# Layer 0's last state-space group: its squares summed on TensorE in the output product's PSUM bank, and a later share of the GLU stream

## The chip, the cores and the metric

The program runs on one core of a Trainium2 chip. Its time is the device time of one execution in microseconds (us). The engines are TensorE (PE; its weight loads are PEld), VectorE (DVE), ScalarE (ACT), GpSimd (POOL) and SyncE (SP), whose queue issues most of the transfers.

## The reference

Four layers act on a residual stream of 4 sequences of 512 tokens with 256 features. Layer 0 is a Mamba-2 mixer and then a SwiGLU. Only this part is changed:

```python
proj = einsum('bld,pd->blp', x, W_in)            # 2048 gate, 2304 x/B/C, 32 dt
hBC  = silu(causal_conv4(...)); xs, B, C = split(hBC)
dt   = softplus(dt + dt_bias);  dA = exp(-exp(A_log) * dt)
h_t  = dA_t * h_(t-1) + (dt_t * x_t) outer B_t   # 32 heads of 64, state 128
y    = (h . C) + D * xs
g    = y * silu(gate)
g    = g * rsqrt(mean(g*g over 2048) + 1e-5) * norm_w
out  = einsum('bli,di->bld', g, W_out)
```

Layer 1 is a latent attention and a product-key mixture with its own GLU; layers 2 and 3 are not touched.

## The kernel before

Tokens lie in 16 tiles of 128, four to a sequence. Everything is fp32.

**The mixer** is the generator `mamba_pieces`. It works in 16 groups `i` of 8 heads: `b = i // 4` is the sequence, `g = i % 4` the quarter of the heads. A group has four chunks `t` of 128 tokens; chunk (15, 2) below is group 15's third. A chunk takes these steps, by their lines in the profile:

- `before`: transposes of x into a "tr" bank (L429, TensorE), times dt (`xdt`, L431, VectorE).
- `products`: a scan over the decays, `G` (L415, VectorE, in program order).
- `before_gpsimd`, issued one chunk ahead: `G` times C·B (L449, GpSimd) and `xw` (L452, GpSimd).
- `within`: C times the state (L470, TensorE), times `eb` into `y` (L471, VectorE), `y` plus D·x (L472, GpSimd); the state's update (L478 TensorE, L483 and L484 VectorE); the product within the chunk (L488, TensorE), added to `y` (L493) and gated (L494, both VectorE); the squares `sq` of `y` (L496, ScalarE), which GpSimd adds in two halves to the running sums `ssq` (L500, L501; L498 for the sequence's first group).
- `project_out`, one chunk behind: `y` times W_out into a "tr" bank (L509, TensorE), added to `acc` (L515, VectorE).

After a sequence's last chunk TensorE sums `ssq` over the partitions with a column of ones (L520), `rsqrt` is taken of the sums (L90 ScalarE, L91 VectorE), the four tiles of `acc` are scaled into the residual (L152), and `part_done` lets `layernorm` run for that sequence.

While group `i` runs through its chunks, the input products of group `i + 1` (L134 with `w_in`) are made between them. Group 15 has no follower, so no such products lie between its chunks.

**The GLU stream** is `glu_units`: two units of layer 0's GLU for four sequences and the first unit of layer 1's GLU for sequences 0 and 1. A piece is four 128x512 products, gate and up, into "mm" banks (L134 with `wu`), or eight 128x256 products back (L212) into a "tr" bank, added to the residual (L158).

**`weave`** takes the next piece of the stream whose share of its stated total is smaller: 630 for the mixer, 207 for the GLU. Each `yield` names its piece's cost. The tile framework's scheduler then sets the order on each engine; an engine works strictly in that order and waits on semaphores.

**PSUM** has 8 banks: 4 "mm", 2 "tr", 2 "acc" (`Ctx.ps`). **SBUF**: `y` has 3 buffers, `sq` 2, `ssq` 1. The weights of layer 1 are loaded by the SP queue (L53) into memory that layer 0 has given up. ScalarE's queue issues the load of `psw` (L791), which stands ahead of its square root (L90).

Of the kernel before, what the change touches and what calls it, by code (L numbers as in the profile page):

```python
# [15 lines left out]
P = 128  # L16
NB, SEQ, DM = 4, 512, 256
NT = NB * SEQ
NTILE = NT // P
TPB = SEQ // P  # L20
# [62 lines left out]
def v3(ap, b):  # L83
    return ap.rearrange("p (a b) -> p a b", b=b)


def rsqrt(c, pool, out, in_, scale):

    s = c.tile(pool, list(in_.shape), "rsq")
    c.nc.scalar.activation(s, in_, AF.Sqrt, bias=c.eps, scale=scale)  # L90
    c.nc.vector.reciprocal(out, s)  # L91
# [55 lines left out]
def add_scaled(c, t, part, w=None):  # L147

    x = c.x[:, t, :]
    if w is None:  # L150
        return c.nc.vector.tensor_add(x, part, x)
    return c.nc.vector.scalar_tensor_tensor(x, part, w, x, ALU.mult, ALU.add)  # L152
# [93 lines left out]
def mamba_pieces(c, a, ws, open_pool):  # L246
# [4 lines left out]
    nc, tc = c.nc, c.tc  # L251
# [94 lines left out]
    pb, pg2, pool = open_pool("m_b", 2), open_pool("m_g", 2), open_pool("m_t", 2)  # L346
    seqs, groups, chunks, w_in, Gs = {}, {}, {}, {}, {}
# [5 lines left out]
    def sequence(b):  # L353

        tokens = slice(b * SEQ, (b + 1) * SEQ)
        BT = c.tile(pb, [P, SEQ], "BT", bufs=1)
        CT = c.tile(pb, [P, SEQ], "CT")
        for k, out in ((16, BT), (17, CT)):
            pc = c.ps()
            project(c, pc, w_bcd, slice((k - 16) * P, (k - 15) * P), tokens)  # L360
            taps = causal_conv(pool, pc, k, out)
            yield 1.7
            taps()
        pt, pcb = c.ps("tr"), c.ps("acc")
        for t in range(TPB):
            cols = slice(t * P, (t + 1) * P)
            nc.tensor.transpose(pt[:, cols], BT[:, cols], c.ident)
            nc.tensor.matmul(pcb[:, cols], lhsT=BT[:, cols], rhs=CT[:, cols], start=True, stop=True)
        Btok = c.tile(pb, [P, TPB, P], "Btok")
        CB = c.tile(pb, [P, TPB, P], "CB")  # L370
        nc.scalar.copy(Btok, v3(pt, P))
        nc.scalar.copy(CB, v3(pcb, P))
        acc = c.tile(pb, [P, TPB, DM], "acc")
        ssq = c.tile(pb, [P, TPB, 2, P], "ssq", bufs=1)
        seqs[b] = CT, Btok, CB, acc, ssq
        yield 1.3
# [68 lines left out]
    def before_gpsimd(i, t):  # L445
        b, g = i // 4, i % 4
        chunk = chunks[i, t]
        G, xdt = chunk[:2]
        nc.gpsimd.tensor_mul(G, G, seqs[b][2][:, t, :][:, None, :].to_broadcast([P, HG, P]))  # L449
        if t < TPB - 1:  # L450
            chunk[2] = xw = c.tile(pool, [P, 512], "xw")
            nc.gpsimd.tensor_mul(  # L452
                v3(xw, HD), v3(xdt, HD), by_head(after[:, b * TPB + t, g * HG : (g + 1) * HG])
            )

    state = {}

    def within(i, t):

        b, g = i // 4, i % 4  # L460
        CT, Btok, CB, acc, ssq = seqs[b]
        G, xdt, xw, xD, eb = chunks.pop((i, t))
        tt, hs, cols = b * TPB + t, slice(g * HG, (g + 1) * HG), slice(t * P, (t + 1) * P)
        y = c.tile(pool, [P, 4, P], "y", bufs=3)
        if t > 0:
            S = state[i]
            yb = c.ps("acc")
            for k in range(4):
                ks = slice(k * P, (k + 1) * P)
                nc.tensor.matmul(yb[:, ks], lhsT=S[:, ks], rhs=CT[:, cols], start=True, stop=True)  # L470
            nc.vector.tensor_mul(y, v3(yb, P), eb)  # L471
            nc.gpsimd.tensor_add(y, y, xD)  # L472
        n = 4 * i + t + 1
        if n < 64:
            before_gpsimd(n // 4, n % 4)
        if t < TPB - 1:
            pst = c.ps()
            nc.tensor.matmul(pst, lhsT=Btok[:, t, :], rhs=xw, start=True, stop=True)  # L478
            if t == 0:
                S = state[i] = c.tile(pool, [P, 512], "S")  # L480
                nc.scalar.copy(S, pst)
            else:
                nc.vector.tensor_mul(v3(S, HD), v3(S, HD), by_head(etot[:, tt, hs]))  # L483
                nc.vector.tensor_add(S, pst, S)  # L484
        ya = c.ps("acc")
        for h in range(HG):
            part = slice(h % 2 * HD, (h % 2 + 1) * HD)
            mm = nc.tensor.matmul(  # L488
                ya[part, h // 2 * P : (h // 2 + 1) * P],
                lhsT=xdt[:, h * HD : (h + 1) * HD], rhs=G[:, h, :], start=True, stop=True,  # L490
            )
            tc.keep_in_program_order(mm)
        tc.keep_in_program_order(nc.vector.tensor_add(y, v3(ya, P), y if t > 0 else xD))  # L493
        nc.vector.tensor_mul(y, y, groups[i][3][:, :, cols])  # L494
        sq = c.tile(pool, [P, 4, P], "sq")
        nc.scalar.activation(sq, y, AF.Square)  # L496
        if g == 0:
            nc.gpsimd.tensor_add(ssq[:, t], sq[:, :2], sq[:, 2:])  # L498
        else:
            nc.gpsimd.tensor_add(ssq[:, t], ssq[:, t], sq[:, :2])  # L500
            nc.gpsimd.tensor_add(ssq[:, t], ssq[:, t], sq[:, 2:])  # L501
        return y

    def project_out(i, t, y):
        b, g = i // 4, i % 4
        acc, ssq = seqs[b][3:]
        po = c.ps("tr")[:, :DM]
        for k in range(4):
            nc.tensor.matmul(  # L509
                po, lhsT=y[:, k, :], rhs=groups[i][1][:, k, :], start=(k == 0), stop=(k == 3)  # L510
            )
        if g == 0:
            nc.scalar.copy(acc[:, t, :], po)
        else:
            nc.vector.tensor_add(acc[:, t, :], po, acc[:, t, :])  # L515
        if g == 3 and t == TPB - 1:
            pss = c.ps()[:, :TPB]
            for u in range(TPB):
                for k in range(2):
                    nc.tensor.matmul(  # L520
                        pss[:, u : u + 1], lhsT=ssq[:, u, k, :], rhs=c.ones[:, :1],
                        start=(k == 0), stop=(k == 1),
                    )
            rs = c.tile(pb, [P, TPB], "rs")
            c.eps = c.eps5
            rsqrt(c, pb, rs, pss, 1.0 / 2048.0)
            for u in range(TPB):
                add_scaled(c, b * TPB + u, acc[:, u, :], rs[:, u : u + 1])
            c.part_done(b)
# [19 lines left out]
    behind = None  # L549
    for i in range(16):  # L550
        for t in range(TPB):
            if t == 1 and i % 4 == 3 and i < 15:
                yield from sequence(i // 4 + 1)
            taps = []
            for k in ((0, 1), (2,), (3,), ())[t] if i < 15 else ():
                taps.append(group(i + 1, k))
                yield 3.4
            n = 4 * i + t + 1
            if n < 63:
                decays((n + 1) // 4, (n + 1) % 4)  # L560
            if n < 64:
                before(n // 4, n % 4)
            yield 0.5
            for tap in taps:
                tap()
            y = within(i, t)
            if n < 63:
                products(n + 1)
            yield 2.6
            if behind:  # L570
                project_out(*behind)
                yield 1.7
            behind = i, t, y
    project_out(*behind)


# [28 lines left out]
def layer0(c, a, x_in, con):  # L605

    with ExitStack() as stack:
        open_pool = lambda name, bufs, **kw: stack.enter_context(
            c.tc.tile_pool(name=name, bufs=bufs, **kw)
        )  # L610
        c.weights = open_pool("m_w", 1)
        unit = c.tile(c.weights, [P, 3072], "wu")
        ws = c.tile(open_pool("m_ws", 1), [P, 762], "ws")
        first_loads(c, a, x_in, con, ws, unit)
        for b in range(NB):
            layernorm(c, b)
            c.step(True)
        glu = open_pool("g0", 1)

        def glu_units():  # L620
            same = dict(bufs=5, out_tag="tr")
            yield from glu_pieces(c, glu, [unit], loaded=True, last=False, **same)
            yield from glu_pieces(c, glu, [a["g0_units"][1]], first=1, **same)

            yield from glu_pieces(
                c, glu, [a["g1_units"][0]], last=False, seqs=[0, 1], **same
            )

        c.parts(2, lambda b: layernorm(c, b, c.xn[b * SEQ : (b + 1) * SEQ, :]))
        weave(  # L630
            c,
            (mamba_pieces(c, a, ws, open_pool), 630.0, 0.0),
            (glu_units(), 207.0, 0.0),
        )

# [1220 lines left out]
```

## Time and profile before

| | us |
|---|---|
| median of 3 runs | 3200.73 (3199.61 to 3208.17) |
| the profiled execution | 3132.11 |
| its span | 3130.3 |
| TensorE busy | 3075.6 (98% of the span) |
| VectorE, ScalarE, GpSimd busy | 1816.2, 1258.1, 650.8 |
| granted TensorE clock, mean | 0.993 |

The profiled execution is one run: 1.8 us lie around its span, and it took 68.6 us less than the median of the timed runs. Durations below are of this execution. TensorE's ends are modelled, so starts are the safer figures. An fp32 product shows as two records, so "x8" is four products. "Waits" lists who waited for whom; the "timeline" lists instructions in order with the idle time before them in brackets; "windows" give busy time and granted clock of a stretch.

### The profile page before, as it was taken

To read this page: it belongs to the slowest core of one execution; us is meant where nothing else is said; L and a number is where in the kernel's file an instruction comes from. 1 tells how busy PE (TensorE), PEld (TensorE's weight loads), DVE (VectorE), ACT (ScalarE), POOL (GpSimd) and SP (SyncE) were. 2 spreads that over 40 slices of the span, in tenths; PEclk is the share of its full clock that TensorE was granted. 3 is DMA by queue.
4 is the path that set the end of the run, shared out by engine and by line. 5 is a ranking of instruction groups with operands and counts; after the bars stand their busy time and mean duration, and the time that the engine had idled before them with its cause. 6 is when DMAs were issued, how large, how long until landed. Compare 5 with 4: busy or idle time off the path is not lost.

```text
span 3130.3 us, 35680 instructions
## 1 busy us (share of the span) xinstructions
PE 3075.6 (98%) x12502; PEld 1886.1 (60%) x12502; DVE 1816.2 (58%) x4644; ACT 1258.1 (40%) x2916; POOL 650.8 (21%) x517
## 2 busy tenths in 40 slices
PE   8999999999899999999999999999999999999999
PEld 5566566566656555555676656656566655555555
DVE  5777778777777787777656555455555422222222
ACT  4434435444466666667425433333333311111111
POOL 0465655556300133331233000000000000000000
PEclk9999999999999999999899999999999999999999
DMA  3233323232221154543232000000000000000000
GB/s 124 86 101 121 100 93 111 85 124 87 88 60 52 45 132 96 127 120 116 66 110 88 1 21 8 1 28 1 21 1 1 21 21 21 21 21 21 0 0 27
DMA packets 89090, 185.12 MB, mean 59 GB/s; under 512 B 14192, under 2 KB 57216, under 8 KB 84176
## 3 DMA queue, kind: packets, MB, share of 16 engines
q1 hardware_dynamic: 74448, 135.05, 13.4%
q0 software_dynamic: 14176, 47.01, 6.1%
q8 instruction: 99, 1.62, 0.2%
q10 hardware_dynamic: 288, 0.79, 0.1%
q14 instruction: 79, 0.65, 0.1%
HBM read 160.92 MB, written 12.98 MB: 56 GB/s over the span
## 4 chain that ended last, share of the span: by engine, by line
PE 87%; DVE 7%; POOL 2%; ACT 2%; DMA 1%; issue 1%; SPq 0%; ACTq 0%; DVEq 0%; POOLq 0%
PE mm L134 34%; PE acc L212 9%; PE mm L655 8%; PE mm L142 5%; PE acc L1165 4%; PE acc L671 4%; PE tr L509 3%; PE tr L1157 2%; PE tr L782 2%; PE tr L212 2%; PE acc L918 2%; PE acc L488 1%; PE mm L1495 1%; PE acc L932 1%; DVE cy L280 1%
## 5 line engine op out<-in xcount | busy, mean ns | idle before, releaser
L134 PE MATMUL mm<-xnT,wu 128*128 128x512 f32 x2128 | 951.2, 595 | 0.2
L134 PEld LDWEIGHTS mm<-xnT,wu 128*128 128x128 f32 x2128 | 400.4, 191 | 461.9 <-issue 438.5
L662 ACT ACTIVATE pr<-pr,nm 128x128 f32<-128x128 f32 (+3 forms) x512 | 285.7, 558 | 294.7 <-DVE nm L658 292.3
L202 DVE TENSOR_TENSOR hT<-sg,mm 128x512 f32<-128x512 f32 x176 | 120.4, 684 | 393.4 <-PE mm L134 388.4
L201 ACT ACTIVATE sg<-mm 128x512 f32<-128x512 f32 x176 | 104.6, 595 | 579.7 <-PE mm L134 579.5
L658 DVE CUSTOM_DVE_ANT_0 pr<-mm,late 128x128 f32<-128x128 f32 (+3 forms) x512 | 245.4, 482 | 93.4 <-PE mm L655 91.1
L212 PE MATMUL acc<-wu,hT 128*128 128x256 f32 x1280 | 287.1, 380 | 1.4 <-DVE x L158 1.4
L212 PEld LDWEIGHTS acc<-wu,hT 128*128 128x128 f32 x1280 | 241.4, 190 | 49.6 <-issue 17.2
L1036 POOL DMA_INDIRECT e<-in_p_experts,ids x128 | 130.7, 1021 | 477.9 <-DVE x L152 354.3
L134 PE MATMUL mm<-xnT,w_in 128*128 128x512 f32 x512 | 228.5, 593 | 0.1
L280 DVE SCALAR_TENSOR_TENSOR cy<-mm,ws,cy 128x509 f32<-128x509 f32 (+2 forms) x216 | 159.7, 745 | 65.4 <-ACT cy L276 61.8
L655 PE MATMUL mm<-kf,qf 128*128 128x128 f32 (+3 forms) x512 | 178.9, 449 | 2.3 <-DVE nm L658 1.3
L655 PE MATMUL mm<-k,q 128*128 128x128 f32 (+3 forms) x512 | 176.5, 434 | 1.0 <-DVE q L1130 1.0
L449 POOL TENSOR_TENSOR G<-G,CB 128x1024 f32<-128x1024 f32 x64 | 152.8, 2388 | 93.7 <-DVE G L415 93.7
L435 ACT ACTIVATE xD<-xc,ws 128x128 f32<-128x128 f32 x256 | 84.1, 391 | 196.2 <-POOL y L472 186.6
L134 PEld LDWEIGHTS mm<-xnT,w_in 128*128 128x128 f32 x512 | 96.7, 190 | 107.9 <-issue 101.5
L152 DVE SCALAR_TENSOR_TENSOR x<-acc,cw,x 128x256 f32<-128x256 f32 x128 | 61.9, 483 | 153.7 <-PE acc L212 153.6
L1165 PE MATMUL acc<-PT,V 128*128 128x512 f32 (+3 forms) x512 | 149.1, 433 | 0.0
L415 DVE TENSOR_TENSOR_SCAN G<-G,eye 128x1024 f32<-128x1024 f32 x64 | 146.8, 2295 | 0.0
L1130 DVE TENSOR_SCALAR q<-mm,bias 128x512 f32<-128x512 f32 x64 | 48.0, 750 | 165.2 <-PE mm L134 165.2
L782 PEld LDWEIGHTS tr<-con,pr 128*128 128x128 f32 x640 | 81.4, 143 | 90.9 <-ACT pr L775 29.1
L782 PE MATMUL tr<-con,pr 128*128 128x128 f32 x640 | 122.8, 283 | 10.1 <-ACT PT L786 4.7
(337 smaller groups left out, 4936.1 us busy)
## 6 DMA issues: line engine op xcount, KB each, us to landing
G<-own SPq DMA_DIRECT2D x64, 512.0 KB, 4.2
w_in<-in_m_units SPq DMA_DIRECT2D x16, 1024.0 KB, 5.4
eb<-since SPq DMA_DIRECT2D x96, 128.0 KB, 4.0
wu<-in_o_units SPq DMA_DIRECT2D x8, 1536.0 KB, 6.7
wo<-in_m_units SPq DMA_DIRECT2D x16, 512.0 KB, 3.8
psw<-pes SPq DMA_DIRECT2D x128, 64.0 KB, 3.2
wu<-in_g_units SPq DMA_DIRECT2D x4, 1536.0 KB, 6.9
wu<-in_f_units SPq DMA_DIRECT2D x4, 1536.0 KB, 7.3
```

The costliest lines, as they stand in the source:

```text
L134: c.nc.tensor.matmul(out, lhsT=w[:, d, cols], rhs=c.xnT[:, d, tokens], start=(d == 0), stop=(d == 1))
L142: c.nc.tensor.matmul(out, lhsT=c.xnT[:, d, tokens], rhs=w[:, d, cols], start=(d == 0), stop=(d == 1))
L212: nc.tensor.matmul(po[:, j, :], lhsT=hT[k][:, (t + j) * P : (t + j + 1) * P], rhs=wd[:, k, :], start=(i == 0), stop=(i == per - 1),)
L280: nc.vector.scalar_tensor_tensor(y[:, j:], src[:, : SEQ - j], conv[:, k, 3 - j : 4 - j], y[:, j:], ALU.mult, ALU.add,)
L415: tc.keep_in_program_order(nc.vector.tensor_tensor_scan(flat, flat, eye.rearrange("p h t -> p (h t)"), 0.0, ALU.mult, ALU.add))
L449: nc.gpsimd.tensor_mul(G, G, seqs[b][2][:, t, :][:, None, :].to_broadcast([P, HG, P]))
L655: nc.tensor.matmul(sc, lhsT=q[:, i * P : n], rhs=k[:, :n], start=True, stop=True)
L658: nc.vector.tensor_tensor_reduce(out=pr, in0=sc, in1=late[:, SEQ - n :], scale=1.0, scalar=-NEG, op0=ALU.add, op1=ALU.min, accum_out=nm,)
L662: nc.scalar.activation(pr, pr, AF.Exp, bias=nm, scale=-1.0, accum_out=total)
L782: nc.tensor.transpose(pt[:, (i - j) * P : (i - j + 1) * P], prs[s][i][:, j * P : (j + 1) * P], c.ident)
L1036: nc.gpsimd.indirect_dma_start(out=e, out_offset=None, in_=a["p_experts"], in_offset=bass.IndirectOffsetOnAxis(ap=ids[:, t, k : k + 1], ax ...
L1165: nc.tensor.matmul(z[:, j * P :], lhsT=head["V"][:, j, h, :], rhs=head["PT"][:, j, j * P :], start=(j == 0), stop=(j == TPB - 1),)
```

## The change

There are three edits, all in layer 0.

1. In group 15 alone, GpSimd no longer adds the squares to `ssq`. Instead `project_out` sums, for each chunk, the two blocks of `ssq` (groups 12 to 14) and the four blocks of `sq` with six products of one column, in column 256 of the bank that holds that chunk's output product. ScalarE copies the column to a new tile `sums`, from which `rsqrt` reads.
2. In group 15, two yields of each chunk name 2.5 more, and the mixer's total in `weave` goes from 630 to 650, so that the GLU stream moves later against the mixer, and goes on during group 15.
3. The third GLU unit (layer 1's) takes its L212 banks from "mm" and not from "tr".

```diff
-    state = {}
+    state, sums = {}, []
...
         if g == 0:
             nc.gpsimd.tensor_add(ssq[:, t], sq[:, :2], sq[:, 2:])
-        else:
+        elif i < 15:
             nc.gpsimd.tensor_add(ssq[:, t], ssq[:, t], sq[:, :2])
             nc.gpsimd.tensor_add(ssq[:, t], ssq[:, t], sq[:, 2:])
-        return y
+        return y, sq
...
-    def project_out(i, t, y):
+    def project_out(i, t, y, sq):
         b, g = i // 4, i % 4
         acc, ssq = seqs[b][3:]
-        po = c.ps("tr")[:, :DM]
+        bank = c.ps("tr")
+        po = bank[:, :DM]
...
             nc.vector.tensor_add(acc[:, t, :], po, acc[:, t, :])
+        if i == 15:
+            if t == 0:
+                sums.append(c.tile(pb, [P, TPB], "sums", bufs=1))
+            parts = [ssq[:, t, k, :] for k in range(2)] + [sq[:, k, :] for k in range(4)]
+            for k, part in enumerate(parts):
+                nc.tensor.matmul(
+                    bank[:, DM : DM + 1], lhsT=part, rhs=c.ones[:, :1], start=(k == 0),
+                    stop=(k == 5),
+                )
+            nc.scalar.copy(sums[0][:, t : t + 1], bank[:, DM : DM + 1])
         if g == 3 and t == TPB - 1:
-            pss = c.ps()[:, :TPB]
+            if i == 15:
+                pss = sums[0]
+            else:
+                pss = c.ps()[:, :TPB]
...
-            yield 0.5
+            alone = 2.5 if i == 15 else 0.0
+            yield 0.5 + alone
...
-            y = within(i, t)
+            y, sq = within(i, t)
...
-            yield 2.6
+            yield 2.6 + alone
...
-                c, glu, [a["g1_units"][0]], last=False, seqs=[0, 1], **same
+                c, glu, [a["g1_units"][0]], last=False, seqs=[0, 1], bufs=5, out_tag="mm"
...
-            (mamba_pieces(c, a, ws, open_pool), 630.0, 0.0),
+            (mamba_pieces(c, a, ws, open_pool), 650.0, 0.0),
```

In the changed file the six products are L523, the copy is L527, and L509 and L515 become L510 and L516; below, L509 and L515 keep their old names.

## Prediction

> **What bounds the kernel now.** The page first: TensorE is busy nearly throughout, so only its own work and the holes in it count.
>
> ```profile
> PE 3075.6 (98%) x12502; PEld 1886.1 (60%) x12502; DVE 1816.2 (58%) x4644; ACT 1258.1 (40%) x2916; POOL 650.8 (21%) x517
> ```
>
> Next the windows, to find the holes. In layer 0 they lie at its start (75 to 100 us) and, most of all, at its end. TensorE's busy time and clock there:
>
> ```profile
> 780.00:785.00 5.00, 2.98 (x26) 1.86 (x24) 3.35 (x3) 2.38 (x6) 2.81 (x3) 1.00 0.68 201
> 785.00:790.00 5.00, 4.40 (x13) 3.64 (x14) 4.96 (x6) 1.47 (x4) 4.92 (x4) 0.68 0.16 57
> ...
> 800.00:805.00 5.00, 3.41 (x25) 2.29 (x24) 5.00 (x6) 0.74 (x2) 3.87 (x3) 1.00 0.00 0
> 805.00:810.00 5.00, 2.52 (x14) 2.30 (x16) 4.39 (x6) 0.63 (x1) 2.75 (x2) 0.73 0.47 131
> ```
>
> The first pair after the length is TensorE, the fifth GpSimd, then the clock. TensorE has holes, and its clock falls after them, while GpSimd is nearly full. Third, TensorE's timeline at these places, with each hole and its releaser:
>
> ```profile
> 785.60 2.66 PE L509 MATMUL tr<-wo,y 128*128 128x256 f32 x8 [2.62 <-DVE acc L515]
> ...
> 802.82 1.99 PE L509 MATMUL tr<-wo,y 128*128 128x256 f32 x8 [1.41 <-DVE acc L515]
> 807.48 2.07 PE L470 MATMUL acc<-CT,S 128*128 128x128 f32 x8 [2.66 <-DVE S L484]
> ...
> 812.90 1.40 PE L520 MATMUL mm<-con,ssq 128*128 128x1 f32 x12
> ...
> 816.91 0.60 PE L520 MATMUL mm<-con,ssq 128*128 128x1 f32 x4 [0.35 <-POOL ssq L501]
> ...
> 825.07 1.13 PE L142 MATMUL mm<-wu,xnT 128*128 128x256 f32 x4 [1.85 <-DVE sg L166]
> ```
>
> The four holes before 818 add up to 7.04 us. At half clock, 785.60 to 792.7 and 807.48 to 811.07, the groups took 2.66, 4.68, 2.07 and 1.66 us where their full-clock neighbours take 1.99, 3.62, 1.06 and 1.09: 3.3 us lost. VectorE is only the messenger. Fourth, GpSimd's and VectorE's timelines:
>
> ```profile
> 801.06 1.92 POOL L500 TENSOR_TENSOR ssq<-ssq,sq 128x256 f32<-128x256 f32 x1 [2.26 <-ACT sq L496]
> 803.05 0.73 POOL L501 TENSOR_TENSOR ssq<-ssq,sq 128x256 f32<-128x256 f32 x1
> 803.74 2.35 POOL L449 TENSOR_TENSOR G<-G,CB 128x1024 f32<-128x1024 f32 x1
> ```
> ```profile
> 803.88 2.75 DVE L483 TENSOR_TENSOR S<-S,etot 128x512 f32<-128x512 f32 x1
> ```
>
> GpSimd idles for a chunk's squares with the next G behind it, and L483 (0.68 us at 770.23, when alone) ends only as L449 ends; the state, L484 and TensorE's L470 come after it. The bound of group 15 is thus the loop through GpSimd.
>
> **What the Trainium skill says.** "SBUF — State Buffer", section "SBUF: two separate sides": VectorE with two SBUF inputs and GpSimd hold one port pair exclusively, each for a whole instruction. The trace agrees (2.75 against 0.69 above). "TensorE: Matmul & The Clock Gate", Part 1: an idle window of about 3.4 us halves the clock until a busy window has passed. The trace shows half clock for about 3.3 us, but after idle stretches of only 2.62 and 2.66 us. "PSUM — Partial Sum Buffer", the rule under bank collisions: guard by bank, not by address. No trace here shows a collision, but in the built program the first L523 of each chunk does wait for that chunk's L515, which reads the same bank.
>
> **The change part by part.** I set the built order of the changed program against these durations. Zero is the start of L429 after the last `w_in` products, 767.63 in the trace.
>
> 1. *GLU pieces moved.* Before, two L212 blocks (3.45 us each) lie after zero. In the changed order it is two `wu` blocks (3.5 each) and two L212 blocks: 13.9 against 6.9, so zero itself comes 7.0 us earlier. On TensorE alone this is work moved, not saved; it pays by filling holes.
> 2. *L500, L501 of group 15 gone.* Eight instructions, about 10 us on GpSimd (0.73 to 2.70 each), off the loop. Chunk (15, 0)'s own G is not helped, since group 14's sums stay.
> 3. *L523 added.* Each chunk has six products of one column, 12 records; 12 records of L520 took 1.40 us. Four chunks: 5.6, less the four removed pairs (8 products, 1.9): +3.7 us on TensorE.
> 4. *Filling.* TensorE's work from zero to the last L523, from row starts (L429 0.44, L470 0.89, L478 0.95, L488 1.03, L509 1.83, blocks as above, 1.4 per six L523, 1.9 for layer 1's first products), is 50.8 us. Before, the end of L520 is at 817.51, that is 49.9, of which 39.5 is work at full clock; 39.5 + 7.0 + 3.7 + 0.9 for a product now ahead gives about the same.
> 5. *Waits that remain.* The 2.62 hole goes: y of (14, 3) is done at 15.4 as before, but TensorE comes to L509 at 18.8, not 15.3, since a `wu` block lies ahead. The L484 hole goes: the second L212 covers it. **A new wait appears**: L523 of (15, 0) stands ahead of L488 and L212 on TensorE and waits for L515 of (15, 0), which VectorE makes only after L493, L494 and the 2.28 us scan. TensorE gets there at 31.5, L515 ends at about 33.8: 2.5 us with the semaphore, with L488, the second L212 and the next L470 queued behind, and through L488 VectorE's L493. The later three L523 groups have 5 to 6 us or other products ahead; I give them and the last y together 0.9. Total 54.2.
> 6. *End of the squares.* 54.2 less 7.0 is 47.2 against 49.9: **2.7 us earlier**.
> 7. *After it.* ScalarE now makes a copy (0.3), and its `psw` issue (1.59 before, then beside the wait), table load (1.28) and root come in line behind: squares to root about 3.5 us, against 2.3. From the root VectorE still needs 4.5 us to L166. So the L142 that waited 1.85 us is reached 2.7 - 1.3 = **1.4 us earlier**, with a longer hole, about 4 us, since only 4.3 us of products (6.0 before) cover it.
> 8. *Start of layer 0.* The total of 650 also reorders its start: the first L212 now comes after the transposes, so VectorE's L158 no longer stands ahead of a convolution tap and the two scans. They began at 90.82 and may begin about 1.4 us sooner; at the end of that chain TensorE waited 3.54 us for `xw`. I take **1.4 us** (bounds 0 and 3.5).
> 9. *Costed at nothing.* Elsewhere in layer 0 the pieces shift by up to two; TensorE's other waits from 110 to 765 are 7 us in all, so at most that is gained, and as much may be lost: plus or minus 3. The GLU's weight loads (6.9 us to land) have over 12 us of products between last and first use. ScalarE's copies fit its idle time. Banks: L212 on "mm" competes with four products, no `w_in` among them after zero. The SP queue's L53 for layer 1 now also waits for the second L212 (39.9), first used at 47: covered by 7 us for a 385 KB load that goes first. Layers 1 to 3 keep their order.
>
> Sum: 1.4 + 1.4 = 2.8 us gained. The two half-clock stretches are already in the sum as gone; the new holes of 2.5 and about 4 us are of the size that brought them, and each would cost at most 1.65. I let them cost 0.3 together, since the later work also waits for other engines there, and take 2.5: 3129.6 for the profiled execution in place of 3132.11. The timed runs lie 68.6 us higher, I assume unchanged: **3198.2 us**.
>
> **Rivals.** A difference of 0.3% (9.6 us) is about what a measurement of this kernel can tell from no change.
>
> *Clean fill* (0.22): the L523 wait proves short, VectorE being freed of the port conflicts; all of 7.04 + 3.3 - 3.7 = 6.6 us at the end and 3.5 at the start are gained, 10.1, and with it some small waits: 3189. For it: GpSimd's 10 us. Against: the scan stands ahead of L515 in VectorE's order.
>
> *The bank's wait becomes the bound* (0.16, slower): each L523 waits for its L515, at 2.5 us in four places 10 us, three new half-clock stretches 5, and 3.7 of products, 18.7, against 10.3 taken away: 8.4 us longer, 3209; with the longer root, 1.3, 3210.4, just past 0.3%. It decides if TensorE comes to every L523 over 2 us before VectorE's L515. For it: the order. Against: L212 and L509 lie between in (15, 1).
>
> *It doesn't do what it says*: the GLU stream would run dry before group 15. The built order speaks against it, with four blocks after zero; this lies within the likeliest case, near 3201.
>
> **How the numbers follow.** The likeliest case (0.62), with plus or minus 3 for the other waits, 1.65 for each half-clock stretch and the bounds of the start, reaches 3191.5 to 3207 and lies within 0.3%. Faster by over 0.3% is the clean fill, 0.22; slower the bank's wait, 0.16. The range for 8 in 10, stretched to most of both rivals: 3186 to 3211.
>
> **What would show it.** In the profile after: no hole at the L509 of (14, 3); no L500 or L501 in group 15; L523 six times four, about 1.4 us each; a hole of some 2.5 us at the first L523, released by L515; L483 near 0.7 us in chunk (15, 2); a longer hole at L142 after the root, released by L166; the wait for `xw` near 100 us down to about 2. I am wrong if the end of the squares comes over 5 us earlier or any later than before, if TensorE's other waits in layer 0 grow by more than 3 us, or if the time moves in layers 1 to 3.

## The result, and the profile after

The changed kernel takes 3198.87 us (median of 22 runs, 3193.73 to 3209.55), the kernel before 3205.04 beside it (22 runs, 3196.41 to 3214.94). The ratio is 0.9979, 95% interval 0.9971 to 0.9986: **6.7 us faster (4.5 to 9.3)**, within the 0.3% that the prediction called no change. The forecast was 2.5 us.

The page of the kernel after, engines (lines after L507 carry numbers one to seventeen higher than before: L509 is L510, L515 is L516, L791 is L808):

```profile
PE 3099.3 (97%) x12534; PEld 1898.2 (59%) x12534; DVE 1820.1 (57%) x4644; ACT 1257.2 (39%) x2918; POOL 637.9 (20%) x509
```

TensorE has the 32 added records (12534 against 12502), GpSimd eight instructions fewer. This execution is 72 us longer than the one profiled of before. That is not the change's doing: layers 1 to 3, whose instructions are the same, took between 2246 and 2321 us in the traces of this study whatever the kernel (2321.3 us here, 2250.1 in another trace of the same changed kernel), and the kernel before has a median of 3131 us in one group of runs and of 3193 to 3205 in the others. So the traces are compared in layer 0.

Windows there (length, then TensorE, weight loads, VectorE, ScalarE, GpSimd; then the clock, the DMA share and GB/s):

```profile
785.00:790.00 5.00, 5.00 (x37) 3.84 (x36) 4.90 (x7) 0.00 (x0) 3.46 (x2) 1.00 0.00 1
790.00:795.00 5.00, 2.67 (x17) 1.75 (x15) 3.60 (x4) 1.91 (x5) 1.58 (x2) 1.00 0.19 55
795.00:800.00 5.00, 4.40 (x33) 3.86 (x34) 4.53 (x7) 0.16 (x1) 4.03 (x2) 0.81 0.00 0
...
825.00:830.00 5.00, 5.00 (x17) 2.84 (x16) 3.17 (x9) 2.14 (x11) 0.00 (x0) 0.66 0.31 105
```

The holes of group 15 are gone at 785, but a new one stands at 790 to 795, and the clock is low after it and again at 825. TensorE's timeline of the kernel after names them (start, length, engine, line, operation, tiles, form, records, and in brackets the idle time ahead and what ended it):

```profile
795.60 0.61 PE L523 MATMUL tr<-con,ssq 128*128 128x1 f32 x4 [2.93 <-DVE acc L516]
796.07 1.03 PE L523 MATMUL tr<-con,sq 128*128 128x1 f32 x8
797.03 1.09 PE L488 MATMUL acc<-G,xdt 128*64 128x128 f32 x16
798.05 5.41 PE L212 MATMUL mm<-wu,hT 128*128 128x256 f32 x16
...
814.90 1.02 PE L134 MATMUL mm<-xnT,wu 128*128 128x512 f32 x2
815.76 0.50 PE L523 MATMUL tr<-con,ssq 128*128 128x1 f32 x4
816.12 1.03 PE L523 MATMUL tr<-con,sq 128*128 128x1 f32 x8
...
824.58 1.32 PE L142 MATMUL mm<-wu,xnT 128*128 128x256 f32 x4 [3.02 <-DVE sg L166]
825.70 3.43 PE L134 MATMUL mm<-xnT,wu 128*128 128x512 f32 x4
```

The first L523 waits 2.93 us for L516, which reads its bank. Then L212 takes 5.41 us where 3.62 is usual. The last L523 comes only behind L134. L142 behind the root waits 3.02, and L134 after it takes 3.43 where 1.88 is usual. The start of layer 0 is the other place. TensorE's timeline of the kernel before, then of the kernel after:

```profile
100.81 2.08 PE L478 MATMUL mm<-xw,Btok 128*128 128x512 f32 x2 [3.54 <-POOL xw L452]
102.81 1.71 PE L488 MATMUL acc<-G,xdt 128*64 128x128 f32 x16
```
```profile
103.08 1.12 PE L478 MATMUL mm<-xw,Btok 128*128 128x512 f32 x2 [0.17 <-POOL xw L452]
104.14 1.09 PE L488 MATMUL acc<-G,xdt 128*64 128x128 f32 x16
```

The wait for `xw` has all but gone, and with it the half clock behind it: L478 takes 1.12, not 2.08, and L488 1.09, not 1.71. VectorE's timelines show where it came from: of the kernel before, then of a1, a second trace of the changed kernel whose start is of the same kind as that of the trace of before (see below):

```profile
89.56 0.69 DVE L158 TENSOR_TENSOR x<-tr,x 128x512 f32<-128x512 f32 x1 [0.83 <-PE tr L212]
...
90.82 4.46 DVE L415 TENSOR_TENSOR_SCAN G<-G,eye 128x1024 f32<-128x1024 f32 x2
```
```profile
87.50 4.46 DVE L415 TENSOR_TENSOR_SCAN G<-G,eye 128x1024 f32<-128x1024 f32 x2
...
94.69 0.68 DVE L158 TENSOR_TENSOR x<-tr,x 128x512 f32<-128x512 f32 x1
```

L158, and the wait for TensorE's L212 ahead of it, now stand behind the two scans. VectorE's timeline of the kernel after, chunks (15, 1) and (15, 2):

```profile
788.43 1.02 DVE L483 TENSOR_TENSOR S<-S,etot 128x512 f32<-128x512 f32 x1
...
796.66 1.62 DVE L483 TENSOR_TENSOR S<-S,etot 128x512 f32<-128x512 f32 x1
```

L483 is shorter than before (2.75), but not alone yet: G of the next chunk (L449) still runs beside it.

### The profile page after: what moved, and what is told of

It is laid out like the page before. It is cut to its first block, busy times and chain, and to the rows that moved or that the text cites. A ratio compares the mean times of both kernels' runs of the same rounds, so it can differ in the third digit from the quotient of the medians.

```text
span 3202.2 us, 35743 instructions
## 1 busy us (share of the span) xinstructions
PE 3099.3 (97%) x12534; PEld 1898.2 (59%) x12534; DVE 1820.1 (57%) x4644; ACT 1257.2 (39%) x2918; POOL 637.9 (20%) x509
## 4 chain that ended last, share of the span: by engine, by line
PE 85%; DVE 7%; ACT 2%; POOL 2%; another core or an unknown queue 2%; issue 1%; DMA 1%; SPq 0%; ACTq 0%; DVEq 0%; POOLq 0%
PE mm L134 33%; PE acc L212 8%; PE mm L672 8%; PE mm L142 5%; PE acc L1182 4%; PE acc L688 3%; PE tr L510 2%; PE tr L1174 2%; PE tr L799 2%; PE acc L935 2%; PE acc L949 1%; PE acc L488 1%; PE mm L1512 1%; PE tr L212 1%
## 5 line engine op out<-in xcount | busy, mean ns | idle before, releaser
L134 PE MATMUL mm<-xnT,wu 128*128 128x512 f32 x2128 | 956.5, 597 | 1.1 <-DVE cy L280 0.9
L134 PEld LDWEIGHTS mm<-xnT,wu 128*128 128x128 f32 x2128 | 402.5, 192 | 466.8 <-issue 446.0
L675 DVE CUSTOM_DVE_ANT_0 pr<-mm,late 128x128 f32<-128x128 f32 (+3 forms) x512 | 245.6, 483 | 101.5 <-PE mm L672 89.5
L212 PE MATMUL acc<-wu,hT 128*128 128x256 f32 x1280 | 288.6, 381 | 4.4 <-DVE os L1539 4.4
L212 PEld LDWEIGHTS acc<-wu,hT 128*128 128x128 f32 x1280 | 242.3, 191 | 53.6 <-issue 17.2
L134 PE MATMUL mm<-xnT,w_in 128*128 128x512 f32 x512 | 229.8, 593 | 0.4 <-DVE cy L280 0.4
L449 POOL TENSOR_TENSOR G<-G,CB 128x1024 f32<-128x1024 f32 x64 | 153.1, 2393 | 101.2 <-DVE G L415 98.0
L134 PEld LDWEIGHTS mm<-xnT,w_in 128*128 128x128 f32 x512 | 96.5, 190 | 104.7 <-issue 95.8
```

Of the source, the lines that this page charges most:

```text
L134: c.nc.tensor.matmul(out, lhsT=w[:, d, cols], rhs=c.xnT[:, d, tokens], start=(d == 0), stop=(d == 1))
L212: nc.tensor.matmul(po[:, j, :], lhsT=hT[k][:, (t + j) * P : (t + j + 1) * P], rhs=wd[:, k, :], start=(i == 0), stop=(i == per - 1),)
L675: nc.vector.tensor_tensor_reduce(out=pr, in0=sc, in1=late[:, SEQ - n :], scale=1.0, scalar=-NEG, op0=ALU.add, op1=ALU.min, accum_out=nm,)
```

## A measure for the traces: three stages of layer 0

Each trace is cut at three points: *start*, to TensorE's first L478; *middle*, to its transposes L429 of chunk (15, 0); *end*, to layer 1's first L658 (L675 after) on VectorE; *rest*, to the end. Where the total is 650, one `wu` block and one L212 block (24 records, 7.0 us) lie in the end in place of the middle, so 7.0 is to be added to the middle and taken from the end. The windows of the kernel before and after:

```profile
0.00:100.81 100.81, 88.66 (x337) 50.95 (x337) 57.38 (x115) 51.74 (x83) 8.80 (x9) 1.00 0.33 113
100.81:776.22 675.41, 666.89 (x3190) 416.83 (x3191) 515.43 (x674) 301.51 (x631) 387.27 (x247) 1.00 0.32 102
776.22:879.74 103.52, 92.77 (x455) 62.90 (x453) 72.44 (x172) 48.79 (x141) 42.69 (x46) 0.97 0.30 94
```
```profile
0.00:103.08 103.08, 94.44 (x336) 55.12 (x336) 56.94 (x113) 49.07 (x81) 8.75 (x8) 1.00 0.32 110
103.08:769.77 666.69, 657.90 (x3166) 411.61 (x3167) 520.26 (x675) 301.99 (x631) 386.26 (x247) 1.00 0.32 103
769.77:880.95 111.18, 103.06 (x511) 70.64 (x509) 71.37 (x174) 50.15 (x146) 34.17 (x39) 0.97 0.27 88
```

All traces, in us:

| trace | start | middle | end | rest |
|---|---|---|---|---|
| before | 100.81 | 675.41 | 103.52 | 2250.6 |
| copy of before, b0 | 106.47 | 678.24 | 103.61 | 2246.4 |
| copy of before, b1 | 99.93 | 678.61 | 103.02 | 2308.8 |
| after | 103.08 | 666.69 | 111.18 | 2321.3 |
| copy of after, a0 | 97.86 | 666.73 | 112.70 | 2250.1 |
| copy of after, a1 | 97.50 | 667.07 | 112.42 | 2311.1 |
| squares alone, s1 | 100.17 | 674.86 | 104.75 | 2256.6 |
| total of 650 alone, t1 | 97.34 | 667.41 | 113.33 | 2313.8 |
| GLU's part alone, w1 | 103.00 | 666.75 | 107.99 | 2246.9 |
| the same, w2 | 97.57 | 666.69 | 106.17 | 2311.2 |
| after, squares first, d2 | 97.14 | 666.70 | 107.74 | 2309.1 |
| after, psw on SP, p1 | 103.23 | 667.03 | 111.68 | 2311.4 |
| GLU's part, psw on SP, p2 | 103.12 | 666.82 | 103.09 | 2310.1 |
| squares first, psw on SP, d2p | 96.58 | 666.89 | 101.97 | 2307.5 |

The start has two values some 6 us apart in either kernel (last section), so a start is compared with one of its own kind: about 100.3 against 97.3, or 106.5 against 103.1.

## The experiments

They ran in four groups, each with its own runs of the kernel before beside it: first b0, a0, w1, s1; then a1, d2, p2, d2p; then b1, w2, p1; then t1.

**b0 and b1: the kernel before, unchanged.**

> The kernel before, unchanged. All theories: a ratio of 1 within 0.1%, which shows what the comparison can tell. Its profile is wanted because the execution profiled earlier was 70 us shorter than the timed ones: if the 70 us lie in layers 1 to 3, layer 1's first L832 comes within 1 us of 830.35 as before and the rest later; if they lie in layer 0, L832 comes later too.

> The kernel before, unchanged, once more: 1 within 0.1%. Wanted are its marks in the trace, to be set against those of the changed kernel where the whole kernel takes 3190 us and more: if layers 1 to 3 give the changed kernel the 3 us more that were measured there (6.7 against 2 to 3 in layer 0), this trace takes about 3 us longer than the changed kernel's from the first work of layer 1 to the end; if chance does it, the two are apart by no fixed sign.

Ratios 1.0003 (0.9992 to 1.0015) and 1.0002 (0.9991 to 1.0012). In b0, L832 came at 838.93: 5.7 us of the delay are the start's, some 3 the middle's, so the expected 1 us was wrong. The 3 us are half clock that the same program meets in one execution and not in another. The same wait of 1.99 us stands in the trace of before and in b1, TensorE's timelines:

```profile
497.18 0.66 PE L429 MATMUL tr<-con,xc 128*128 128x128 f32 x4 [1.99 <-ACT xnT L126]
...
498.34 1.02 PE L478 MATMUL mm<-xw,Btok 128*128 128x512 f32 x2
```
```profile
497.54 0.66 PE L429 MATMUL tr<-con,xc 128*128 128x128 f32 x4 [1.99 <-ACT xnT L126]
...
498.70 1.85 PE L478 MATMUL mm<-xw,Btok 128*128 128x512 f32 x2
```

Full clock behind it in one, half clock in the other (the last section says what tells them apart); this is about half of the 3 us, and a longer half clock behind the wait for `xw` is the rest. With a total of 650 the wait of 1.99 is shorter: 1.35 to 1.38 us in all ten such traces, against 1.97 to 1.99 in the four with 630, and half clock followed it in none of the ten and in two of the four. b1's rest is 2.3 us shorter than that of a1, not 3 longer, so these traces show no gain in layers 1 to 3. But the rests of one group lie up to 10 us apart (2246.4 to 2256.6), so they can't rule out a few us there.

**a0 and a1: the changed kernel, unchanged.**

> The changed kernel, unchanged: 2 to 3 parts in a thousand below 1 again, as when first measured (6.7 us, 4.5 to 9.3). If the gain is layer 0's, as both theories of an edit say, then layer 1's first L849 comes 4 us or more ahead of the L832 of the copy of the kernel before. If it is made in layers 1 to 3, whose instructions are the same, the two lie within 1.5 us, as in the first pair of profiles (831.57 against 830.35).

> The changed kernel once more, in the company of the three that follow. Measured so far against the kernel before: 6.7 us faster (4.5 to 9.3) and 0.9 us faster (-2.5 to 4.4). By the marks of the trace in layer 0 it should be 2 to 3 us faster, since layers 1 to 3 have the same instructions; 2 to 5 is expected.

a0: 0.9997 (0.9986 to 1.0008), 0.9 us faster (2.5 slower to 4.4 faster). a1: 0.9979 (0.9972 to 0.9986), 6.7 faster again. a0 missed its expectation in time, and a1 its range of 2 to 5, though in both traces the end is the same within 0.3 us. a0's L849 came at 827.91, 11.0 us ahead of b0's L832, but some 6 of these are the longer start of b0. So the size of the gain is uncertain between these.

**w1 and w2: the GLU's part alone.**

```
-            yield 0.5
+            alone = 2.5 if i == 15 else 0.0
+            yield 0.5 + alone
...
-            yield 2.6
+            yield 2.6 + alone
...
-                c, glu, [a["g1_units"][0]], last=False, seqs=[0, 1], **same
+                c, glu, [a["g1_units"][0]], last=False, seqs=[0, 1], bufs=5, out_tag="mm"
...
-            (mamba_pieces(c, a, ws, open_pool), 630.0, 0.0),
+            (mamba_pieces(c, a, ws, open_pool), 650.0, 0.0),
```

> Only the GLU stream's part (the total of 650, the 2.5 added, the third unit's output on mm); the squares of the last group are still added by GpSimd. Theory GLU: most of the gain, 4 to 8 us, since the hole before L509 of (14, 3), that at L484 and the start's wait for xw are filled by the moved blocks, and no L523 wait exists. Theory GpSimd: at most 2 us, since the loop through GpSimd (L500, L501, L449, L483) still sets the end of the squares, within 1 us of where it was. My prediction's own sum: 1.4 us at the start, and some 2 at the end.

> Only the GLU stream's part, once more. 9.6 us faster than before when first measured (5.9 to 13.1). Theory GLU with the squares' part paying back: again 8 to 13 us faster, and so at least 3 us ahead of the changed kernel's 6.7. If it comes out at 5 to 7, the squares' part costs nothing and the first pair was chance.

w1: 0.9969 (0.9958 to 0.9981), 9.6 us faster, in the group in which the whole change gained 0.9; theory GpSimd, which gave it at most 2, fails. w2: 0.9979 (0.9971 to 0.9987), 6.7 faster. By its own expectation w2 says that the squares' part costs nothing. The traces say otherwise: start and middle are those of the changed kernel, and the end is 108.0 and 106.2 against 111.2 to 112.7, so 3 to 6 us lie in the squares' part. w2's runs fall into two clumps (10 of 22 at 3181.0 to 3185.2, 9 at 3191.1 to 3192.1), and the trace is of the lower; what makes the upper one isn't settled. The two starts, some 6 us apart, may have a part in it, but only one of these executions has a trace. w1 also shows what sets the end then. ScalarE's and TensorE's timelines of w1:

```profile
811.89 2.90 ACTq L792 DMA_DIRECT2D psw<-in_l_rope  x1
814.82 1.28 ACT L90 ACT_TABLE_LOAD   x1 [5.97 <-DMA tok<-xn_tokens]
816.11 0.27 ACT L90 ACTIVATE rsq<-mm,eps 128x4 f32<-128x4 f32 x1
```
```profile
811.25 0.85 PE L520 MATMUL mm<-con,ssq 128*128 128x1 f32 x4
...
821.37 1.16 PE L142 MATMUL mm<-wu,xnT 128*128 128x256 f32 x4 [3.51 <-DVE sg L166]
822.34 3.58 PE L134 MATMUL mm<-xnT,wu 128*128 128x512 f32 x4
```

The sums are there at 812.1, but ScalarE is issuing the load of `psw` until 814.8, then loads the table: the root starts 4.0 us after its input.

**s1: the squares' part alone.** The changed kernel with 630, nothing added, and "tr":

> Only the squares' part: six L523 per chunk, the GLU stream as before (630, nothing added, tr). Theory GpSimd: 4 to 7 us gained, because 10 us of GpSimd leave the loop. Theory GLU: no gain, or up to 4 us lost, since 3.7 us of products are added, the first L523 waits for L515 with nothing new ahead of it, and the holes of 2.62 and about 1.4 stay. My prediction's own sum: the 2.62 hole stays, the hole at L484 goes, 3.7 added: 1 to 3 us slower.

1.0015 (1.0003 to 1.0028): 4.7 us slower (0.9 to 8.8), where theory GpSimd had 4 to 7 us gained. Its end is 104.75 against 103.0 to 103.6. The holes at L510 of (14, 3) and at the first L523 remain; TensorE's timeline of s1:

```profile
784.39 1.99 PE L510 MATMUL tr<-wo,y 128*128 128x256 f32 x8 [2.59 <-DVE acc L516]
...
800.47 0.61 PE L523 MATMUL tr<-con,ssq 128*128 128x1 f32 x4 [1.29 <-DVE acc L516]
```

**t1: the total of 650 alone.** One number of the kernel before:

> The kernel before with the total of 630 made 650 and nothing else: the start is reordered as in the changed kernel, but no 2.5 is added in the last group, so one block of L212 falls into group 15 and one behind the last L520. Theory start: the first scan comes 3.0 to 3.5 us sooner (near 87.3 or, where TensorE begins at half clock for longer, 93.1), and that is the whole gain of this kernel, 2 to 4 us. Theory filling: the holes of group 15 are what pays, and this kernel keeps them (the hole at L484's product and that of the L509 of (14, 3) at 2.6 each), so it gains nothing or loses up to 4, as the last block now stands ahead of layer 1.

0.9985 (0.9976 to 0.9993): 4.8 us faster (2.2 to 7.7). The first scan came at 87.35, as expected, and start and middle are the changed kernel's. Its end, less 7.0, is 106.3, some 3 worse than before: holes of 0.91 to 2.15 us stand in group 15, and L142 waits 3.32 us for L53's load. So the start pays even where group 15 keeps holes.

**d2: the squares ahead of the add.** In the changed kernel the six L523 and the copy move ahead of L516 (they are L519 and L523 then, the add L527):

```
         po = bank[:, :DM]
...
+        if i == 15:
...
+            nc.scalar.copy(sums[0][:, t : t + 1], bank[:, DM : DM + 1])
         if g == 0:
             nc.scalar.copy(acc[:, t, :], po)
         else:
             nc.vector.tensor_add(acc[:, t, :], po, acc[:, t, :])
```

> The changed kernel with the six L523 and their copy written ahead of the add L516 of the same bank: TensorE then has no wait for L516, and each L523 follows its own L510 directly. Theory bank's wait (the squares' part pays back what the GLU's part gains, through the 2.9 us hole at the first L523, the half clock after it, 1.8, and the last L523 issued behind two L134): 4 to 7 us faster than the changed kernel, so 6 to 9 faster than before; the hole at the first L523 is gone and the last of the six ends at least 1 us sooner after the last y. Theory products (it is the added 3.7 us of TensorE, or ScalarE's copy): within 1.5 us of the changed kernel.

0.9964 (0.9950 to 0.9978), 11.5 us faster than before and 5.0 faster than a1 by the medians of one group (3186.5 and 3191.55). The bank's wait is confirmed. TensorE's timeline of d2, chunk (15, 0) and the last chunk:

```profile
782.56 1.99 PE L510 MATMUL tr<-wo,y 128*128 128x256 f32 x8
784.39 0.50 PE L519 MATMUL tr<-con,ssq 128*128 128x1 f32 x4
784.76 1.03 PE L519 MATMUL tr<-con,sq 128*128 128x1 f32 x8
...
803.32 1.03 PE L519 MATMUL tr<-con,sq 128*128 128x1 f32 x8
...
813.90 2.07 PE L142 MATMUL mm<-wu,xnT 128*128 128x256 f32 x4 [3.85 <-DVE sg L166]
```

No wait at the first, and the last ends 4.78 us after the last L494 begins, against 6.66 in the changed kernel. Part of it is lost again: here `psw`'s issue took 2.25 us, the hole at L142 is 3.85, and half clock follows.

**p2, d2p, p1: `psw` issued by SP**, in w1, in d2 and in the changed kernel:

```
-    nc.scalar.dma_start(rope, a["l_rope"])
+    nc.sync.dma_start(rope, a["l_rope"])
```

> Only the GLU's part, and the load of psw issued by SP instead of ScalarE, whose issue stood 2.90 us ahead of the table load and root in the GLU's part alone (0.38 to 1.59 in others). If this issue sets the end: the L142 behind the root is reached about 2.5 us sooner after the last y than with the GLU's part alone (13.96 there), its hole falls from 3.51 to about 1, no half clock follows (1.7), so 3 to 4 us faster than the GLU's part alone, 12 to 14 faster than before. If not, the same as the GLU's part alone, 8 to 10 faster.

> The squares ahead of the add, and psw issued by SP. Theory bank's wait with the issue: the hole at L142 falls under 2.5 us and the half clock behind it goes, 1 to 3 us faster than the squares ahead of the add alone, 8 to 12 faster than before. If GpSimd's relief is worth anything at all, it is here that it shows: this one is then at least as fast as the GLU's part with psw on SP.

> The changed kernel with psw issued by SP instead of ScalarE (0.41 us there, in line between the last copy of the sums and the table load). By sum: the hole at L142 falls from 3.02 to about 2.6 us, and if that no longer brings the half clock (1.3 to 2.1 us), 2 to 2.5 us are gained over the changed kernel, else 0.4. If the gain of the GLU's part with psw on SP over the GLU's part alone were mostly the placing of the table load, this one would gain 1.3 more.

p2: 0.9948 (0.9934 to 0.9961, 5 runs), **16.6 us faster** than before (12.5 to 21.1). d2p: 0.9950 (0.9936 to 0.9964, 5 runs), 16.0 faster. Both gained more than was expected of them, and both beat the changed kernel of their group (0.9979). ScalarE's and TensorE's timelines of p2:

```profile
809.10 1.28 ACT L90 ACT_TABLE_LOAD   x1
812.44 0.27 ACT L90 ACTIVATE rsq<-mm,eps 128x4 f32<-128x4 f32 x1 [2.06 <-PE mm L520]
```
```profile
818.37 1.13 PE L142 MATMUL mm<-wu,xnT 128*128 128x256 f32 x4 [0.27 <-DVE sg L166]
819.34 1.88 PE L134 MATMUL mm<-xnT,wu 128*128 128x512 f32 x4
```

Without the issue in line ScalarE loads its table while it waits, the root follows the sums at once, the hole shrinks to 0.27, and no half clock follows. By the ends of the traces this is worth 3.1 to 4.9 us (103.09 against 106.17 in w2 and 107.99 in w1); the times, taken in different groups, give 7 to 10. p1, where the last copy of the sums stands ahead of the table load, has little of this: the hole is 2.39, half clock follows (L142 1.73), and its end, 111.68, is that of the changed kernel. It measured 0.9991 (0.9982 to 1.0000), 2.9 us faster than before, so the 2 us more that were expected without half clock did not come. Between p2 and d2p lies nothing that the times can tell, and 1.1 us in the end of their traces: that is what GpSimd's relief is worth after the 3.7 us of products that it costs TensorE. What the relief alone is worth was not tested.

## Why the prediction was right, and where it was not

The total lay in the likeliest case and the range held it. That 3198.87 lies 0.7 us from the forecast 3198.2 is luck: the kernel before measured 3205.04 beside it, not 3200.73, and the gain was 6.7 us, not 2.5. Two terms were mis-sized, in opposite directions.

- **Steps 1, 2 and 3** came as counted: 24 records moved, eight instructions less on GpSimd, 32 records more on TensorE, 1.4 us for each six L523.
- **Step 5, the waits.** The 2.62 and 2.66 holes are gone; the new wait at the first L523 is 2.93, taken as 2.5. Right. From the prediction's zero (761.20 in the kernel after, 756.02 in a0, 755.99 in a1) to the end of the last L523 the sum gave 54.2 us; it was 55.95, 57.48 and 57.24. Less the half clock of the next point it is 54.1 in all three: order, costs and waits were right in sum, with the L134 ahead of the last L523 counted (0.9 in step 4).
- **The half clock, charged 0.3, is the term that failed at the end.** From the first L523 to L510 it is 7.70 us in the kernel after and 8.97 in a1, and the same work takes 1.25 + 1.02 + 3.56 = 5.83 in d2: 1.9 and 3.1 us (3.4 in a0). Behind L142 it cost 1.7 in a1 (2.07 + 2.64 against 1.13 + 1.88). So more than was taken from the old half clock (3.3) was paid again. The bound of 1.65 for each hole failed too: in a0 and a1 half clock lasted 6.8 us behind the first hole, twice as long as behind each hole of group 15 before.
- **Step 6, 2.7 us earlier:** not so. From chunk (15, 0)'s transposes to the last squares' product it is 47.4 to 48.9 us, less 7.0 40.4 to 41.9, against 41.3 to 42.2 in the three traces of before. From the prediction's zero, a0 and a1 come later than the 49.9 of the trace of before (50.5 and 50.2), which the prediction had named as a sign that it is wrong.
- **Step 7.** From the squares to the root it took 2.15 us, costed at 3.5, since `psw`'s issue took 0.41, not 1.59. The hole at L142 was 3.02, costed at about 4.
- **The end as a whole**, costed at 1.1 us gained, lost 0.8 to 2.3: 111.2 to 112.7 less 7.0, against 103.4 as the mean of the three.
- **Step 8, the start, failed the other way.** The mechanism was right, L158 left the chain, but the first scan came near 87.3 in place of 90.3 (means among starts of the shorter kind), 3.0 us sooner and not 1.4. The wait for `xw` did not lose 1.4 of its 3.54 us but 3.4, as TensorE's timeline shows, and the half clock behind it, which the sum did not count, went too: 1.6 us in the trace of before (L478 and L488 took 3.65 from start to start there, 2.08 after), more in b1. t1 has the start's gain without the rest.
- **Step 9.** The middle, apart from the half clock, is unchanged: 675.41 - 7.0 - 1.6 = 666.8, against 666.69 in the kernel after. Where b0 and b1 lose 3 us more, half clock does it, as shown above, in part behind a wait that the total of 650 also shortens. Layers 1 to 3 showed no move beyond their spread.

So the sum that the traces give is 3.0 gained at the start, 1.7 to 4.9 of half clock in the middle, and 0.8 to 2.3 lost at the end: 2.4 to 7.1 us gained, where the times gave 6.7, 0.9 (2.5 slower to 4.4 faster) and 6.7. The bank's wait was a true rival: it struck at one L523, not at four, and with the late last L523 cost the 5.0 us that d2 gained back; the start covered it. The clean fill's 10.1 us was come near by w1 (9.6; 6.7 in w2) and passed by d2 (11.5), not by the change. One slip of reading: L483 alone takes 0.68 us, not the 0.69 of the second mention.

Open are the two clumps of w2, and why `psw`'s issue takes 0.38 in one execution and 2.90 in another.

## What to carry to other kernels

When work is moved to fill a hole, look at what else the same number reorders: here a total that was raised for the last group paid at the other end of the layer. Put a product that shares a bank ahead of the engine that reads the bank, not behind it, and follow the in-order issue of a load on the engine whose result is waited for. Count each hole with the slow clock that can come after it, on both sides of the sum: in these traces 1.7 us, or 3.4 where it lasted twice as long.

## What the runs showed of the hardware

- **Half clock behind short holes, but not always.** It followed holes of 2.39 (p1), 2.82 (w2), 2.93 and 3.02 us; it did not follow the 3.02 in s1 (L142 1.13, L134 1.88), and followed 1.99 in b1 but not in the trace of before. The length of one hole does not decide it. Where the hole lies tells the cases apart: within each trace the changes of the granted clock are whole multiples of 3.41 us apart. With stretches cut at these points, the windows around the 1.99 us (length, TensorE, weight loads, VectorE, ScalarE, GpSimd, clock, DMA share, GB/s), of before and then of b1:

```profile
493.24:496.65 3.41, 1.95 (x12) 1.23 (x11) 3.21 (x5) 1.19 (x4) 2.85 (x2) 1.00 0.65 262
496.65:500.06 3.41, 2.88 (x26) 2.13 (x28) 2.08 (x4) 0.96 (x2) 0.95 (x2) 1.00 0.02 10
```
```profile
495.36:498.77 3.41, 1.42 (x13) 1.23 (x12) 2.03 (x4) 1.59 (x3) 1.85 (x2) 1.00 0.23 96
498.77:502.18 3.41, 3.41 (x19) 1.79 (x18) 2.12 (x4) 0.82 (x3) 1.65 (x1) 0.50 0.20 61
```

In b1 the hole falls whole into one stretch, which leaves TensorE busy for 42% of it, and half clock follows; in the trace of before the hole is split, 57% is left, and full clock stays. So too with 3.02 us: s1's is split over two stretches (62% and 50% busy), a1's leaves 12% of one. In layer 0 of the fourteen traces, from 40 us on, 24 such stretches at full clock had TensorE busy for 42% or less, and half clock followed 23 of them. It followed only five busier ones, all at 70 to 74% and each with 1.4 to 1.5 us of the one-column products L520 or L523 in it. An idle stretch of 3.4 us, the rule that the prediction cites, is thus more than was needed here.
- **The first half clock of a kernel has two lengths.** TensorE's timeline of the trace of before, then of b0, the same products:

```profile
16.55 1.10 PE L134 MATMUL mm<-xnT,wu 128*128 128x512 f32 x2
17.49 1.87 PE L142 MATMUL mm<-ws,xnT 128*128 128x32 f32 x16
```
```profile
17.70 2.05 PE L134 MATMUL mm<-xnT,wu 128*128 128x512 f32 x2
19.54 3.46 PE L142 MATMUL mm<-ws,xnT 128*128 128x32 f32 x16
```

It ended before 16.55 us in one and near 27 in the other, which puts the first L478 5.7 us later (some 6 in the means of the kinds), in either kernel: five of the fourteen traces have the longer one. A gain of a few us is best read between marks that lie behind it.
- **A DMA's issue has a price on its engine** that varies: `psw`'s 256 KB took ScalarE 0.38, 0.41 (in four traces), 1.12, 1.59, 2.25, 2.45, 2.50 and 2.90 us.
